# Conditional sequence block: single gathers for the first two tiles, gate weights behind them, gate matmuls as two strips inside the first layer

## The chip, the cores and the metric

The kernel runs on one core of a Trainium2 chip. The metric is the device time of one execution in microseconds (us). A run's profile shows the span from the first to the last instruction; the time of the same execution is somewhat longer. Engines are named as in the profile: PE (TensorE matmul), PEld (TensorE weight load), DVE (VectorE), ACT (ScalarE), POOL (GpSimd), SP (SyncE, which here only issues DMAs). DMA queue q1 is the one that SP issues to, q10 ACT's, q0 POOL's.

## The reference, cut to what matters

`x` is 32 x 128 x 512 float32, `t` 32 x 512, `mask` 32 x 128 (true where a position lies behind the length of its row). Everything is float32.

```python
m = mask[:, :, None]
emb = silu(t) @ ada_w + ada_b                       # 32 x 1536
shift, scale, gate_msa = split(emb, 3, axis=1)
norm = where(m, layernorm(x) * (1 + scale[:, None]) + shift[:, None], 0)
fwd = gelu(norm @ ssm_w1 + ssm_b1) @ ssm_w2 + ssm_b2    # 512 -> 512 -> 512
bwd = gelu(norm @ bwd_w1 + bwd_b1) @ bwd_w2 + bwd_b2    # the two flips cancel
x = x + gate_msa[:, None] * where(m, fwd + bwd, 0)
ff = silu(t) @ ffada_w + ffada_b
shift2, scale2, gate_mlp = split(ff, 3, axis=1)
h = gelu_tanh((layernorm(x) * (1 + scale2[:, None]) + shift2[:, None]) @ ff_w1 + ff_b1)
return x + gate_mlp[:, None] * (h @ ff_w2 + ff_b2)      # 512 -> 1024 -> 512
```

The first half changes only the tokens where the mask is true. The kernel therefore collects those tokens in 512 slots (a loop at the end takes any that are left over), computes the first half for the slots, and puts the results back; the second half is done for all 4096 tokens.

## The kernel before

**Slots.** From the mask, the kernel counts masked tokens per batch row. `edges` holds, for each row, the first slot and the one behind its last (`first`, `behind`), four times over in the 128 partitions. `pick` (128 x 512) is 1 where a slot belongs to a batch row; `pick_slots` (L212) fills half of it. `rank` (32 x 128) holds the rank of each token, and in its last column the number of the row's first token. `tokens_of` (L220) looks slots up: one matmul of `pick` with `rank` for each tile of 128 slots, a comparison with the slot number, a sum, and an addition give the token of each slot as an integer. `gather` (L239) is an indirect DMA on POOL that fetches 128 rows of `x` by these integers. The first two tiles are looked up and gathered together, the other two likewise, later.

**Modulation.** `silu(t)` is transposed to `sT` (128 x 4 x 32). `modulation_matmuls` (L259) multiplies it with the weights `ada_a`, a block of 128 input rows at a time (4 blocks) and a part j of 512 columns (0 shift, 1 scale, 2 gate); part j is written to partitions 32j to 32j+31 of a PSUM tile. `modulation_rows` (L270) adds the biases `modb_a` and so makes the rows of `mod1`. Shift and scale come first (`pm_ss`), the gate (`pm_g`) later, between transposes. `slot_part` (L287, matmul in L282) multiplies 32 rows of `pick` with 32 rows of `mod1` and gives the shift, scale or gate of each slot of a tile (`part_s` in the profile).

**First half.** `statistics` (L149) takes mean and variance (L155 to L158) and, on POOL, the inverse root (L160). `modulated` (L166) does two fused operations of 128 x 512 (L171, L172). `transposed_slots` (L175) transposes a tile in four blocks on PE and copies them with ACT. `hidden` (L182) is the first layer: 8 blocks f of 128 outputs, each 4 matmuls over 256 slots, then a Gelu on ACT with the bias `biasT`; blocks 0 to 3 use `ssm_w1` (`w1[:, :, :512]`), 4 to 7 `bwd_w1`. `project` (L196) is the second layer, `finish_slots` (L295) adds bias, gate and `x` on DVE and stores the rows in DRAM (`x1_rows`). `hidden` for the first two tiles is broken up (L614 to L625): three blocks, the gate of one tile, scale and shift of a later tile, one block, twice.

**Second half.** Two matrix products done with seven instead of eight block products, whose weight sums (`Weights.combine`, L312, and `weight_sums`, L570) DVE computes during the first half. `take_first_half` (L669) gathers the results of the first half from `x1_rows` into tiles of `x` loaded before. Statistics, normalised tiles and transposes follow, and then the block products (L905, L1091) until the end.

**What sets the order.** The opening stands in a manual schedule: each engine does its instructions in the order in which the code writes them. DMA issues wait in the same order on their engine: SP issues nearly all loads and stores, POOL the gathers and the biases, ACT the mask. A DMA also waits when it reuses one of eight completion counters (each next DMA of a kind takes the next) until the DMA before it on that counter has landed. On SP the order is: `t`, four blocks of shift and scale weights, the gate weights (1 MB, L146), then, each after a small memset on POOL that stands behind the gathers (L134), four loads of 1 MB of `w1` and `w2`; then `fw1` (2 MB, L509), `ada_f` (3 MB, L510, into the memory of `ada_a`, hence after the last gate matmul), `b2`, `b2b`, `modb_f`, `fb2`, `fw2` (2 MB, L517) and four loads of `x`. Tile pools rotate: the PSUM pools `ps_t`, `ps_h` and `ps_o` have 2, 3 and 3 banks.

```python
    mv, rstd = statistics(xc, "s01")
    xn_s = [
        modulated(
            xc[c], *rows[c], f"s{c}", xn[:, c], (mv[:, c, 0:1], rstd[:, c : c + 1])
        )
        for c in range(2)
    ]
    modulation_matmuls(pm, ada_a, 2, 3, range(2))
```

Of the kernel before, what the change touches and what calls it, by code (L numbers as in the profile page):

```python
# [22 lines left out]
def kernel(  # L23
# [89 lines left out]

    def broadcast_rows(t, vec, queue):

        n = vec.shape[0] // D
        each = t.shape[0] // n
        for j in range(n):
            queue.dma_start(
                t[j * each : (j + 1) * each, :],  # L120
                vec[ts(j, D)].rearrange("(o d) -> o d", o=1).to_broadcast([each, D]),
            )
# [8 lines left out]
    def load_blocks(t, w):  # L131
        nc.sync.dma_start(t, w.rearrange("(k p) f -> p k f", p=P))
# [5 lines left out]
    modb_a = adap.tile([3 * B, D], F32, tag="modb", name="modb_a", bufs=1)  # L138
# [7 lines left out]
    load_blocks(ada_a[:, :, 2 * D :], ada_w[:, 2 * D :])  # L146


    def statistics(src, name):  # L149

        n = len(src)
        mv = stp.tile([P, n, 2], F32, tag=f"mv{n}", name=f"mv_{name}")
        for i in range(n):
            st = stp.tile([P, 6], F32, tag="st", name=f"st_{name}_{i}")
            nc.vector.bn_stats(st, src[i])  # L155
            nc.vector.bn_aggr(mv[:, i, :], st)
        ve = stp.tile([P, n], F32, tag=f"ve{n}", name=f"ve_{name}")
        nc.vector.tensor_scalar(ve, mv[:, :, 1], EPS, None, ALU.add)  # L158
        rstd = stp.tile([P, n], F32, tag=f"rstd{n}", name=f"rstd_{name}")
        nc.gpsimd.tensor_tensor(rstd, ve, half[:, :n], ALU.pow)  # L160
        return mv, rstd
# [4 lines left out]
    def modulated(src, scale, shift, name, t, stats=None):  # L166

        if stats is None:
            mv, rstd = statistics([src], name)
            stats = mv[:, 0, 0:1], rstd  # L170
        nc.vector.scalar_tensor_tensor(t, src, stats[0], scale, ALU.subtract, ALU.mult)  # L171
        nc.vector.scalar_tensor_tensor(t, t, stats[1], shift, ALU.mult, ALU.add)  # L172
        return t

    def transposed_slots(xn, dst, name):  # L175

        ptr = ps_t.tile([P, 512], F32, tag="tr", name=f"ptr_{name}")
        for k in range(KC):
            nc.tensor.transpose(ptr[:, ts(k, P)], xn[:, ts(k, P)], ident)
        nc.scalar.copy(dst, ptr.rearrange("p (k s) -> p k s", s=P))  # L180
# [31 lines left out]
    def pick_slots(h):  # L212

        part = ts(h, NH)
        nc.vector.tensor_scalar(inside[:, part], slot_row[:, part], behind, None, ALU.is_lt)
        nc.vector.scalar_tensor_tensor(
            pick[:, part], slot_row[:, part], first, inside[:, part], ALU.is_ge, ALU.mult
        )

    def tokens_of(picked, slots, n, name, pool):  # L220

        pl = ps_t.tile([P, 512], F32, tag="tr", name=f"pl_{name}")
        for c in range(n):
            nc.tensor.matmul(pl[:, ts(c, S)], picked[:B, ts(c, P)], rank, start=True, stop=True)
        view = pl[:, : n * S].rearrange("p (c s) -> p c s", s=S)
        before = pool.tile([P, n, S - 1], F32, tag="before", name=f"before_{name}")
        nc.vector.tensor_tensor(
            before,
            view[:, :, : S - 1],
            slots.unsqueeze(2).to_broadcast([P, n, S - 1]),  # L230
            ALU.is_le,
        )
        token = stp.tile([P, n], F32, tag=f"token{n}", name=f"token_{name}", bufs=1)
        nc.vector.tensor_reduce(token, before, axis=AX.X, op=ALU.add)
        token_i = const.tile([P, n], I32, name=f"token_i_{name}")
        nc.vector.tensor_tensor(token_i, token, view[:, :, S - 1], ALU.add)
        return token_i

    def gather(dst, token_col):  # L239
        nc.gpsimd.indirect_dma_start(  # L240
            out=dst,
            out_offset=None,
            in_=x_rows,
            in_offset=bass.IndirectOffsetOnAxis(ap=token_col, axis=0),
        )
# [3 lines left out]
    def find_slots(h):  # L249
        part = slice(h * NC // 2, (h + 1) * NC // 2)  # L250
        return tokens_of(pick[:, ts(h, NH)], slot_col[:, part], NC // 2, f"s{h}", ssm)

    def gather_slots(token_i):
        both = xp.tile([P, 2, D], F32, tag="x", name=f"xc_{len(xc)}")
        for c in range(NC // 2):
            gather(both[:, c], token_i[:, c : c + 1])
            xc.append(both[:, c])

    def modulation_matmuls(pm, ada, lo, hi, blocks):  # L259
        for k in blocks:  # L260
            for j in range(lo, hi):
                nc.tensor.matmul(
                    pm[ts(j, B), :],
                    sT[:, k, :],
                    ada[:, k, ts(j, D)],
                    start=(k == 0),
                    stop=(k == KC - 1),
                )

    def modulation_rows(pm, mod, modb, lo, hi):  # L270
        rows = slice(lo * B, hi * B)
        nc.vector.tensor_tensor(mod[rows], pm[rows], modb[rows], ALU.add)

    def modulation(pm, mod, ada, modb, lo, hi):

        modulation_matmuls(pm, ada, lo, hi, range(KC))
        modulation_rows(pm, mod, modb, lo, hi)

    def of_slots(picked, c, mod, j, pool, tag, name):

        t = pool.tile([P, 512], F32, tag=tag, name=name)
        nc.tensor.matmul(  # L282
            t, picked[ts(j, B), ts(c, P)], mod[ts(j, B), :], start=True, stop=True
        )
        return t

    def slot_part(at, j, pool, tag):  # L287
        return of_slots(pick, at, mod1, j, pool, tag, f"part{j}_s{at}")
# [84 lines left out]
    upper = ssm.tile([B, 2, 4, B], BF16, name="upper")  # L373
# [48 lines left out]
    broadcast_rows(modb_a, ada_b, nc.gpsimd)  # L422
# [30 lines left out]
    pick_slots(0)  # L453

    nc.vector.tensor_scalar(rank[:, : S - 1], pg[:B, : S - 1], first[:B], None, ALU.add)

# [3 lines left out]
    nc.scalar.activation(s_sb, t_sb, AF.Silu)  # L460
    sT = ssm.tile([P, KC, B], F32, name="sT")
# [6 lines left out]

    token_i = find_slots(0)
    gather_slots(token_i)  # L470

    load_behind_gathers(w1[:, :, :D], ssm_w1)
    load_behind_gathers(w1[:, :, D:], bwd_w1)
    load_behind_gathers(w2[:, :KC], ssm_w2)
    load_behind_gathers(w2[:, KC:], bwd_w2)
    for key, vec in (("ssm1", ssm_b1), ("bwd1", bwd_b1), ("ff1", ff_b1)):
        n = vec.shape[0] // P
        nc.gpsimd.dma_start(
            bias_rows[col[key] : col[key] + n, :], vec.rearrange("(c p) -> c p", p=P)
        )  # L480
    pick_slots(1)
# [6 lines left out]
    mod1 = const.tile([3 * B, D], F32, name="mod1")  # L488
    nc.vector.tensor_scalar(modb_a[B : 2 * B], modb_a[B : 2 * B], 1.0, None, ALU.add)
    pm = ps_o.tile([P, 512], F32, tag="o", name="pm_ss")  # L490
    modulation(pm, mod1, ada_a, modb_a, 0, 2)
    rows = [(slot_part(c, 1, ps_o, "o"), slot_part(c, 0, ps_h, "h")) for c in range(2)]
    pm = ps_o.tile([P, 512], F32, tag="o", name="pm_g")
# [3 lines left out]
    mv, rstd = statistics(xc, "s01")  # L497
    xn_s = [
        modulated(
            xc[c], *rows[c], f"s{c}", xn[:, c], (mv[:, c, 0:1], rstd[:, c : c + 1])  # L500
        )
        for c in range(2)
    ]
    modulation_matmuls(pm, ada_a, 2, 3, range(2))
# [10 lines left out]
    for t, vec in ((b2, ssm_b2), (b2b, bwd_b2), (modb_f, ffada_b), (fb2, ff_b2)):  # L515
        broadcast_rows(t, vec, nc.sync)
    nc.sync.dma_start(fw2, ff_w2.rearrange("(k p) f -> p k f", p=P))  # L517
    x_of = {0: load_x(0)}
    transposed_slots(xn_s[0], xT_s[:, :, ts(0, P)], "s0")
    modulation_matmuls(pm, ada_a, 2, 3, range(2, 3))  # L520
    token_i = find_slots(1)
    gather_slots(token_i)
    transposed_slots(xn_s[1], xT_s[:, :, ts(1, P)], "s1")
    modulation_matmuls(pm, ada_a, 2, 3, range(3, KC))
# [6 lines left out]
    modulation_rows(pm, mod1, modb_a, 2, 3)  # L531

    every = ssm.tile([B, 2, P], BF16, name="every")
# [80 lines left out]
    for c in range(2):  # L614
        h1 += hidden(xT_s, NH, w1, 0, AF.Gelu, "s0", ssm, range(4 * c, 4 * c + 3))
# [21 lines left out]
    fw2_of.combine(0, 1)  # L637
# [7 lines left out]
    modulation(pm, mod2, ada_f, modb_f, 0, 3)  # L645
# [3 lines left out]
    gs = [keep_gate(c, slot_part(c, 2, ps_o, "o")) for c in (2, 3)]  # L649
# [720 lines left out]
    with tc.If(more > 0):  # L1370
# [11 lines left out]
        with tc.For_i(0, more, 1):  # L1382
# [4 lines left out]
            tok_i = tokens_of(pick_l, col_l, 1, "l", lp)  # L1387
# [7 lines left out]
            for half_no, (mod, was, wbs, bias, bcol, func) in enumerate(  # L1395
                (
                    (mod1, (ssm_w1, bwd_w1), (ssm_w2, bwd_w2), b2, col["ssm1"], AF.Gelu),
                    (mod2, (ff_w1,), (ff_w2,), fb2, col["ff1"], AF.Gelu_apprx_tanh),
# [10 lines left out]
                scale = of_slots(pick_l, 0, mod, 1, ps_o, "o", f"sc_l{half_no}")  # L1409
                shift = of_slots(pick_l, 0, mod, 0, ps_h, "h", f"sh_l{half_no}")  # L1410
# [5 lines left out]
                gate_l = of_slots(pick_l, 0, mod, 2, ps_h, "h", f"gate_l{half_no}")  # L1416
# [60 lines left out]
```

## Time and profile before

| what | value |
|---|---|
| three runs | 464.16, 466.93, 466.88 us; median 466.88 |
| the profiled execution | 463.4 us, span 461.7 us |
| busy in the span: PE, PEld, DVE | 448.6 us (97%), 364.2 (79%), 332.1 (72%) |
| ACT, POOL | 175.2 (38%), 157.8 (34%) |
| DMA | 70.41 MB, mean 153 GB/s |
| chain that ended last, by engine | PE 69%, DVE 9%, ACT 7%, POOL 5%, SP's queue 4%, issue 4% |

A timeline line gives start, length, engine, line of the code, operation, output and inputs, shapes and the number of instructions; in brackets stands the idle time of the engine before it and what ended it. A float32 matmul shows as two records. Matmul ends are modelled, so a busy PE may also be waiting. Tiles that are numbered in the code (`ssm_w1`, `h_s0`) lose their numbers in the profile; `w` is `w1` or `w2`, `fw` is `fw1` or `fw2`.

### The profile page before, as it was taken

To read this page: it belongs to the slowest core of one execution; us is meant where nothing else is said; L and a number is where in the kernel's file an instruction comes from. 1 tells how busy PE (TensorE), PEld (TensorE's weight loads), DVE (VectorE), ACT (ScalarE), POOL (GpSimd) and SP (SyncE) were. 2 spreads that over 40 slices of the span, in tenths; PEclk is the share of its full clock that TensorE was granted. 3 is DMA by queue.
4 is the path that set the end of the run, shared out by engine and by line. 5 is a ranking of instruction groups with operands and counts; after the bars stand their busy time and mean duration, and the time that the engine had idled before them with its cause. 6 is when DMAs were issued, how large, how long until landed. Compare 5 with 4: busy or idle time off the path is not lost.

```text
span 461.7 us, 5825 instructions
## 1 busy us (share of the span) xinstructions
PE 448.6 (97%) x2000; PEld 364.2 (79%) x2000; DVE 332.1 (72%) x538; ACT 175.2 (38%) x380; POOL 157.8 (34%) x153
## 2 busy tenths in 40 slices
PE   6899999999999999999999999999999999999995
PEld 2385385677888888788888888888888888888884
DVE  4649868999678839986787498867873995434645
ACT  3121021744445361344455513444455144562000
POOL 6210083048980000489700005987000025660000
PEclk9999999999999999999999999999999999999999
DMA  8999835692207734833077258220872342222022
GB/s 276 386 407 361 307 136 88 204 346 88 106 5 224 105 84 137 297 100 130 1 229 114 69 182 298 92 87 14 226 108 67 134 163 79 81 85 98 0 85 101
DMA packets 82418, 70.41 MB, mean 153 GB/s; under 512 B 63168, under 2 KB 63696, under 8 KB 81362
## 3 DMA queue, kind: packets, MB, share of 16 engines
q1 hardware_dynamic: 67298, 57.03, 39.4%
q0 software_dynamic: 4480, 11.66, 7.1%
q10 hardware_dynamic: 10608, 1.32, 2.0%
q8 instruction: 17, 0.28, 0.2%
q14 instruction: 15, 0.12, 0.1%
HBM read 56.83 MB, written 13.17 MB: 152 GB/s over the span
## 4 chain that ended last, share of the span: by engine, by line
PE 69%; DVE 9%; ACT 7%; POOL 5%; SPq 4%; issue 4%; DMA 1%; POOLq 0%; ACTq 0%; DVEq 0%
PE a_m L905 15%; PE a_o L1091 14%; PE e_m L905 12%; PE e_o L1091 12%; PE ph_s L188 6%; PE po_s L202 4%; SPq L744 4%; POOL hb L989 2%; ACT hb L867 2%; ACT xT L727 1%; DVE sx L834 1%; DVE xT L725 1%; ACT ha L867 1%; DVE xn_sy L838 1%; PE part_s L282 1%
## 5 line engine op out<-in xcount | busy, mean ns | idle before, releaser
L956 POOL TENSOR_TENSOR ha<-p_m,ha 128x512 f32<-128x512 f32 x20 | 26.9, 1345 | 152.5 <-ACT ha L963 143.3
L1091 PE MATMUL e_o<-fw,ha 128*128 128x256 f32 x256 | 57.9, 379 | 0.0
L727 ACT ACTIVATE xT<-xT,modT 128x128 f32<-128x128 f32 x112 | 44.1, 480 | 30.5 <-DMA xT<-xn 30.3
L1091 PE MATMUL a_o<-t,hb 128*128 128x256 f32 x240 | 54.1, 379 | 0.0
L1091 PEld LDWEIGHTS e_o<-fw,ha 128*128 128x128 f32 x256 | 48.6, 190 | 6.6
L1091 PEld LDWEIGHTS a_o<-t,hb 128*128 128x128 f32 x240 | 45.6, 190 | 6.2
L673 POOL DMA_INDIRECT x<-x_rows,slot_i x32 | 36.4, 1136 | 28.7 <-DMA x_rows<-t_s 18.1
L867 ACT ACTIVATE hb<-hb,biasT 128x256 f32<-128x256 f32 x64 | 29.0, 501 | 27.8 <-POOL hb L989 19.3
L956 POOL TENSOR_TENSOR hb<-p_m,hb 128x512 f32<-128x512 f32 x20 | 28.2, 1409 | 20.4 <-DVE hb L935 20.1
L919 ACT COPY p_m<-e_m 128x512 f32<-128x512 f32 x27 | 15.8, 585 | 49.2 <-PE e_m L905 46.8
L1091 PE MATMUL e_o<-fw,s 128*128 128x256 f32 x128 | 29.2, 381 | 0.5 <-DVE s L1039 0.3
L963 ACT COPY ha<-e_m 128x512 f32<-128x512 f32 x32 | 18.5, 578 | 28.0 <-PE e_m L905 27.7
L1091 PE MATMUL a_o<-t,s 128*128 128x256 f32 x128 | 28.9, 379 | 0.0
L1091 PE MATMUL a_o<-fw,ha 128*128 128x256 f32 x128 | 28.9, 379 | 0.0
L202 PE MATMUL po_s<-w,h_s 128*128 128x512 f32 x64 | 28.6, 593 | 0.0
L188 PE MATMUL ph_s<-xT_s,w 128*128 128x256 f32 x128 | 28.6, 382 | 0.0
L1091 PEld LDWEIGHTS e_o<-fw,s 128*128 128x128 f32 x128 | 24.1, 190 | 4.8 <-DVE s L1039 1.7
L188 PEld LDWEIGHTS ph_s<-xT_s,w 128*128 128x128 f32 x128 | 24.0, 190 | 4.7 <-ACT h_s L192 1.5
L1091 PEld LDWEIGHTS a_o<-t,s 128*128 128x128 f32 x128 | 24.3, 190 | 3.3
L1091 PEld LDWEIGHTS a_o<-fw,ha 128*128 128x128 f32 x128 | 24.3, 190 | 3.3
L867 ACT ACTIVATE ha<-e_m,biasT 128x256 f32<-128x256 f32 x48 | 20.0, 468 | 15.5 <-PE e_m L905 10.2
L930 DVE TENSOR_TENSOR e_m<-a_m,ha 128x512 f32<-128x512 f32 x20 | 13.9, 697 | 16.6 <-POOL ha L956 6.6
(210 smaller groups left out, 870.3 us busy)
## 6 DMA issues: line engine op xcount, KB each, us to landing
tw<-t_rows SPq DMA_DIRECT2D x16, 896.0 KB, 4.7
x<-in_x_dram SPq DMA_DIRECT2D x16, 512.0 KB, 8.4
gate<-gate_rows POOLq DMA_DIRECT2D x8, 1024.0 KB
out_dram<-x SPq DMA_DIRECT2D x15, 512.0 KB, 3.1
xT<-xn SPq DMA_DIRECT2D x92, 64.0 KB, 2.4
fw<-in_L_cond_ff_w_dram SPq DMA_DIRECT2D x2, 2048.0 KB
ada_f<-in_L_cond_ffada_w_dram SPq DMA_DIRECT2D x4, 768.0 KB, 13.7
ada_a<-in_L_cond_ada_w_dram SPq DMA_DIRECT2D x4, 512.0 KB, 5.9
```

Source lines behind the costliest of these rows:

```text
L188: nc.tensor.matmul(ph[:, :n], w[:, k, ts(f, P)], xT[:, k, :], start=(k == 0), stop=(k == KC - 1))
L202: nc.tensor.matmul(po, h[f][:, ts(i, P)], w[:, f, :], start=(f == 0), stop=(f == HC - 1))
L673: nc.gpsimd.indirect_dma_start(out=xs[i // G][i % G // 2][:, i % 2], out_offset=None, in_=x1_rows[:slots, :], in_offset=bass.IndirectOffse ...
L727: nc.scalar.activation(out, src, AF.Identity, bias=shift, scale=scale)
L744: queues[b % len(queues)].dma_start(dst[ts(q, R), b], src[ts(b, R), q])
L867: nc.scalar.activation(dst[:, n], src[:, n], AF.Gelu_apprx_tanh, bias=biasT[:, f : f + 1])
L905: nc.tensor.matmul(bank[:, ts(n, QT)], self.w_block(j, product)[:, ts(n, P)], self.x_block(j, product), start=(product in ("P1", "P5") and ...
L919: nc.scalar.copy(p5, e)
L930: nc.vector.tensor_tensor(e, a, p5, add)
L956: nc.gpsimd.tensor_tensor(self.place(RESULT[j], c), self.p5[j], other, ALU.add)
L963: nc.scalar.copy(self.place(RESULT[j], c), src)
L1091: nc.tensor.matmul(part, src[:, k, ts(i, P)], w[product][:, k, :], start=(last and k == 0), stop=True, skip_group_check=True,)
```

## The change

- The first two tiles are picked, looked up, compared and gathered each on its own (`pick_slots(ts(0, P))`, `find_slots` for one tile, `gather_slots`); the two look-up matmuls still stand together.
- The gate weights move on SP from before the gathers to behind the first half of `ssm_w1`, which alone keeps its memset on POOL. `ssm_w1` is loaded in two halves.
- The three bias vectors are loaded by ACT's queue instead of POOL's, behind the Silu.
- Statistics of tile 0 stand ahead of the addition of the shift and scale rows on DVE, those of tile 1 behind it.
- The second modulating operation of tile 1, its transposes and its copies are done in two pieces.
- The gate matmuls leave the places between the transposes. They stand between blocks 1 and 2 of the first layer and go alternately to partitions 64 to 95 and 96 to 127, so that their sum is in two strips. `mod1` and `modb_a` have 32 rows more (zeros in the bias, by a memset on DVE), and a slot's gate is a product over 64 rows, which adds the strips.
- Look-up and gathers of tiles 2 and 3 stand ahead of the transposes of tiles 0 and 1.
- `fw2` is loaded behind two of the four loads of `x`; `fw2_of.combine(0, 1)` moves behind the rows of `mod2`; the gate of tile 3 takes a bank of `ps_h`.

```diff
-    modb_a = adap.tile([3 * B, D], F32, tag="modb", name="modb_a", bufs=1)
+    modb_a = adap.tile([4 * B, D], F32, tag="modb", name="modb_a", bufs=1)
...
     ada_a = load_ada(ada_w, "a", 2 * D)
-    load_blocks(ada_a[:, :, 2 * D :], ada_w[:, 2 * D :])
...
-    def modulated(src, scale, shift, name, t, stats=None):
+    def modulated(src, scale, shift, name, t, stats=None, pieces=1):
...
-        nc.vector.scalar_tensor_tensor(t, t, stats[1], shift, ALU.mult, ALU.add)
+        for q in range(pieces):
+            part = ts(q, D // pieces)
+            nc.vector.scalar_tensor_tensor(
+                t[:, part], t[:, part], stats[1], shift[:, part], ALU.mult, ALU.add
+            )
...
+    def look_up(pl, picked, blocks):
+        for n, c in enumerate(blocks):
+            nc.tensor.matmul(pl[:, ts(n, S)], picked[:B, ts(c, P)], rank, start=True, stop=True)
+
+    def tokens_of(pl, slots, n, name):
...
+    def strip(pm, n, ada, k, j, start, stop):
+
+        nc.tensor.matmul(
+            pm[ts(n, B), :], sT[:, k, :], ada[:, k, ts(j, D)], start=start, stop=stop
+        )
...
-    broadcast_rows(modb_a, ada_b, nc.gpsimd)
+    nc.vector.memset(modb_a[3 * B :], 0.0)
+    broadcast_rows(modb_a[: 3 * B], ada_b, nc.gpsimd)
...
-    pick_slots(0)
+    pick_slots(ts(0, P))
 
     nc.vector.tensor_scalar(rank[:, : S - 1], pg[:B, : S - 1], first[:B], None, ALU.add)
-
+    pick_slots(ts(1, P))
...
+    for key, vec in bias_vecs:
+        n = vec.shape[0] // P
+        nc.scalar.dma_start(
+            bias_rows[col[key] : col[key] + n, :], vec.rearrange("(c p) -> c p", p=P)
+        )
...
-    token_i = find_slots(0)
-    gather_slots(token_i)
-
-    load_behind_gathers(w1[:, :, :D], ssm_w1)
-    load_behind_gathers(w1[:, :, D:], bwd_w1)
-    load_behind_gathers(w2[:, :KC], ssm_w2)
-    load_behind_gathers(w2[:, KC:], bwd_w2)
...
+    look_up(pl, pick, range(2))
+    for c in range(2):
+        gather_slots(both, c, find_slots(pl[:, ts(c, S)], c, 1))
+
+    load_behind_gathers(w1[:, :, : D // 2], ssm_w1[:, : D // 2])
+    load_blocks(ada_a[:, :, 2 * D :], ada_w[:, 2 * D :])
+    load_blocks(w1[:, :, D // 2 : D], ssm_w1[:, D // 2 :])
+    load_blocks(w1[:, :, D:], bwd_w1)
+    load_blocks(w2[:, :KC], ssm_w2)
+    load_blocks(w2[:, KC:], bwd_w2)
+    pick_slots(ts(1, NH))
...
+    mod = const.tile([4 * B, D], F32, name="mod1")
+    mod1 = [(ts(0, B), mod), (ts(1, B), mod), (ts(1, 2 * B), mod)]
     nc.vector.tensor_scalar(modb_a[B : 2 * B], modb_a[B : 2 * B], 1.0, None, ALU.add)
+    mv = stp.tile([P, 2, 2], F32, tag="mv2", name="mv_s01")
+    moments(xc[0], mv[:, 0, :], "s0")
     pm = ps_o.tile([P, 512], F32, tag="o", name="pm_ss")
-    modulation(pm, mod1, ada_a, modb_a, 0, 2)
+    modulation(pm, mod, ada_a, modb_a, 2)
+    moments(xc[1], mv[:, 1, :], "s1")
+    rstd = deviations(mv, "s01")
     rows = [(slot_part(c, 1, ps_o, "o"), slot_part(c, 0, ps_h, "h")) for c in range(2)]
-    pm = ps_o.tile([P, 512], F32, tag="o", name="pm_g")
+    pl = ps_h.tile([P, 512], F32, tag="h", name="pl_2")
+    look_up(pl, pick, range(2, 4))
...
+    both = xp.tile([P, 2, D], F32, tag="x", name="xc_2")
+    gather_slots(both, 0, find_slots(pl[:, : 2 * S], 2, 2))
...
+    x_of = {0: [load_side(0, 0)]}
     nc.sync.dma_start(fw2, ff_w2.rearrange("(k p) f -> p k f", p=P))
-    x_of = {0: load_x(0)}
-    transposed_slots(xn_s[0], xT_s[:, :, ts(0, P)], "s0")
-    modulation_matmuls(pm, ada_a, 2, 3, range(2, 3))
-    token_i = find_slots(1)
-    gather_slots(token_i)
-    transposed_slots(xn_s[1], xT_s[:, :, ts(1, P)], "s1")
-    modulation_matmuls(pm, ada_a, 2, 3, range(3, KC))
+    x_of[0].append(load_side(0, 1))
+    for c in range(2):
+        transposed_slots(xn[:, c], xT_s[:, :, ts(c, P)], f"s{c}", 1 + c)
...
-        h1 += hidden(xT_s, NH, w1, 0, AF.Gelu, "s0", ssm, range(4 * c, 4 * c + 3))
+        h1 += hidden(xT_s, NH, w1, 0, AF.Gelu, "s0", ssm, range(4 * c, 4 * c + 2))
+        if c == 0:
+            pm = ps_o.tile([P, 512], F32, tag="o", name="pm_g")
+            for k in range(KC):
+                strip(pm, 2 + k % 2, ada_a, k, 2, k < 2, k > 1)
+            nc.vector.tensor_tensor(mod[2 * B :], pm[2 * B :], modb_a[2 * B :], ALU.add)
+        h1 += hidden(xT_s, NH, w1, 0, AF.Gelu, "s0", ssm, range(4 * c + 2, 4 * c + 3))
...
-    fw2_of.combine(0, 1)
...
-    gs = [keep_gate(c, slot_part(c, 2, ps_o, "o")) for c in (2, 3)]
+    gs = [
+        keep_gate(2, slot_part(2, 2, ps_o, "o")),
+        keep_gate(3, slot_part(3, 2, ps_h, "h")),
+    ]
+    fw2_of.combine(0, 1)
```

## The prediction

> **What bounds the kernel now.** I read the engine totals first, then the chain of work that ended last, then the timeline of the first 90 us, then the DMA queues microsecond by microsecond.
>
> The table of stretches (columns: stretch, its length, then busy time of PE, PEld, DVE, ACT, POOL) says that TensorE is the bound once it has started:
>
> ```profile
> 20.00:25.00 5.00, 5.00 (x24) 3.57 (x23) 2.04 (x6) 1.23 (x3) 2.35 (x3) 1.00 1.05 392
> 50.00:60.00 10.00, 10.00 (x46) 4.11 (x45) 6.78 (x11) 1.17 (x2) 1.63 (x2) 1.00 0.68 258
> 60.00:70.00 10.00, 10.00 (x48) 8.81 (x47) 7.35 (x16) 2.84 (x6) 8.28 (x9) 1.00 0.29 105
> 100.00:200.00 100.00, 98.98 (x450) 84.23 (x449) 80.84 (x125) 44.38 (x98) 40.92 (x35) 1.00 0.48 142
> ```
>
> So the end moves by when the first layer (`ph_s`) starts, plus whatever work is put on PE behind that. The timeline (start, length, engine, line) shows what `ph_s` waited for:
>
> ```profile
> 7.86 1.05 POOL L240 DMA_INDIRECT xc<-in_x_dram,token_i_s  x1 [3.30 <-DVE inside L215]
> 9.22 0.97 POOL L240 DMA_INDIRECT xc<-in_x_dram,token_i_s  x1 [0.30 <-issue]
> 10.79 1.05 PE L262 MATMUL pm_ss<-ada_a,sT 128*32 128x512 f32 x4 [0.22 <-DMA ada_a<-in_L_cond_ada_w_dram]
> 11.89 0.68 DVE L272 TENSOR_TENSOR mod<-pm_ss,modb_a 64x512 f32<-64x512 f32 x1 [1.46 <-PE pm_ss L262]
> 14.03 0.69 DVE L155 BATCH_NORM_STATS2 st_s<-xc 128x6 f32<-128x512 f32 x1 [1.45 <-DMA xc<-in_x_dram,token_i_s]
> 14.55 1.90 PE L262 MATMUL pm_g<-ada_a,sT 128*32 128x512 f32 x4
> 14.86 0.66 DVE L155 BATCH_NORM_STATS2 st_s<-xc 128x6 f32<-128x512 f32 x1
> 18.30 0.75 DVE L172 SCALAR_TENSOR_TENSOR xn_s<-xn_s,rstd_s,part_s 128x512 f32<-128x512 f32 x1
> 20.38 1.04 PE L262 MATMUL pm_g<-ada_a,sT 128*32 128x512 f32 x2
> 21.59 5.45 PE L188 MATMUL ph_s<-xT_s,w 128*128 128x256 f32 x24
> 33.28 1.23 DVE L316 TENSOR_TENSOR t<-fw 128x1024 f32<-128x1024 f32 x1 [2.12 <-DMA fw<-in_L_cond_ff_w_dram]
> 52.76 3.63 PE L262 MATMUL pm_f<-ada_f,sT 128*32 128x512 f32 x24
> 58.07 1.08 POOL L673 DMA_INDIRECT x<-x_rows,slot_i  x1 [18.15 <-DMA x_rows<-t_s]
> ```
>
> VectorE idles until the first gather lands at 14.0, 5.1 us after its descriptors were written (8.91). Then it is one chain to 21.59, with gate matmuls and a look-up between the transposes. The queues say why the gather is late. From 10 to 11 us the hardware queue, still moving gate weights, has the engines to itself; from 12 to 13 the gather runs:
>
> ```profile
> q1 hardware_dynamic: 183, 0.37, 102.9%
> q0 software_dynamic: 1, 0.00, 0.1%
> ```
>
> ```profile
> q0 software_dynamic: 96, 0.34, 89.8%
> q1 hardware_dynamic: 40, 0.06, 16.2%
> ```
>
> **The change, part by part.**
>
> *Look-ups and gathers.* Compare, pick, count on 128 instead of 256: row 215 is 0.35 us at 256, row 216 0.48 at 256, and 512-wide forms of that kind take 0.74, so 1 ns an element: 0.22 and 0.35; rows 227 and 234 go from 0.42 to 0.29. Rank is ready at 4.88 instead of 5.07, the second pick at 5.48. In the new instruction order the first compare waits for both look-up matmuls, so it starts at 5.62+0.60 (row 224: 1.20 for two)+0.1=6.3, not 6.51. Token 0 is there at 7.10 instead of 7.58. Gathers are issued at 7.38 and 8.73 instead of 7.86 and 9.22: 0.5 us.
>
> *Gate weights behind them.* The mixing-weight blocks were moved by 9.0 (2.1 MB summed over q1); a gather behind an empty queue starts within 0.9 us of its descriptors (the one written at 59.15 has packets between 59 and 60). So tile 0 moves from about 9.2 to 9.9 and, with the 1.3 us between the last packets and use (12.7 to 14.0), lands at 11.2; tile 1 (written 9.70) at about 12.2. Bounds: 10.5 with no queue in front, 13.5 if the 5.1 us lag stays. I take 11.2, as the row at 12 to 13 us shows the gather at full rate as soon as q1 is empty.
>
> *New wait.* On VectorE the statistics of tile 0 now stand ahead of the addition that ends `pm_ss`. 11.2+0.93 gives 12.15 for the addition, not 11.89; the four `part_s` matmuls wait behind it. The second statistics start at 12.86 instead of 14.86.
>
> *From there to the first layer.* Before: 14.86 to the last modulation 18.30 is 3.44. Now its first half (0.48) and second (0.47), two transposes (0.33), a 256-wide copy (0.37 between 0.27 at 128 and 0.58 at 512) and hand-overs make the bias transpose free at 4.77 and `ph_s` at 5.00 after the statistics: 17.86. Its third block of rows is ready at 5.24, and is needed at 5.86. First layer 21.59-17.86=3.73 us earlier. First weights: half of `w1`, issued at 10.0, needs 2 us to start and 1.4 us of data, landed about 14; gate weights about 17, used from 21.3; nothing waits.
>
> *Strips.* Four gate matmuls leave the waiting time and go between blocks 1 and 2 on the bound engine. Row `pm_f`: 24 records in 3.56 with three strips side by side, 0.445 per pass; two strips, four passes: 1.78. Upper bound, no overlap: the row at 14.55, 1.90 for two, so 3.8. I take 1.8, nearest in form. Net so far 3.73-1.8=1.9 us.
>
> *Queues.* The three bias loads leave POOL (0.5 us each at 10.3, nothing waiting) for ACT between 3.33 and the copy of `sT` at 4.87; that copy may slip 0.3 and is wanted at 6.2. SP: `ada_f` waits for the gate strips (23 us instead of 21.45), with everything behind it; the 2 MB of `fw` keep the queue full to 33, so nothing. `fw2` behind two x loads lands near 51 and is used at 55: nothing. One more memset on DVE before 2.87: idle anyway. The subtraction moved behind `mod2` (2.45) fills DVE's idle at 55.2 (1.3) and 57.2 (1.7); nothing waits for `modT` before 80. The last gate part takes a `ps_h` bank, so its matmul need not wait for VectorE's addition at 52.94 (that addition was done before the four at 56.33 ran, 1.98 us in one go): nothing gained, and the bank is copied out before block 2 asks for it. Three memsets less on POOL (four took 0.31) and the earlier gathers let the first weights go at 10.0, not 10.49.
>
> *What is late next.* Between 9.0 and 12 q1 has nothing queued but the gathers (0.52 MB, 1.35 us): against before some 1.1 us of DMA time is lost, and the queue is full from there to 53.5. `fw` lands at about 34.3, not 33.2, and VectorE works from it without a pause: 33.28 to 52.91, less the moved 2.48, is 17.15 us, so the last addition for slots starts at 51.5, where PE alone would allow 51.0. Its store runs behind the queue's end (54.6), lands at 56.7, and the gathers start at 56.7 instead of 58.07: 1.35 earlier. That chain ends in the normalised tile at 79.46, which PE transposes at 79.50, with about 0.25 us to spare. So 1.6 of the 1.9 us are kept.
>
> The profiled execution took 463.4 (span 461.7, 1.7 around it): it would be 461.8. Runs shown are 464.16, 466.88, 466.93; against the median 466.88-1.6=**465.3 us**.
>
> [...] The early `pm_ss` passes are 0.85 us apart, `pm_f`'s 0.43, though the granted clock stands at 1.00 in both: PE warmed up near 9 us. [...]
> [...]
>
> **Rivals.**
> 1. *Slower: the gather keeps its lag.* If the 5.1 us are the gather's own, tile 0 lands at 13.5, now ahead of the `pm_ss` addition: 14.45, statistics 15.15, `ph_s` 20.15, plus 1.8 is 0.4 later than before; at 14.0 it is 0.9: 467.3 to 467.8. It decides from a landing at 13.1 (13.1+0.95+0.7+5.0+1.8=21.6). For it: the later gathers, 2.9 us from descriptors to packets at 22 to 25. Against it: that queue was full.
> 2. *Strips serial, or PE slow again.* Serial strips cost 3.8 against 3.73: no change, 466.9. Against: `pm_f`. If `ph_s` began at the pace of `pm_ss` between 6.33 and 9.0 (2.7 us at half pace), 1.35 of the 1.9 would go: 466.3. Against: PE is never idle for a whole microsecond in 14.5 to 17.9.
> 3. *Given back later.* If the queue ends 2 us later instead of 1.1, the gathers at 58.07 gain 0.5 only: 466.2. For: the queue is full to 53.5.
> 4. *More.* Tile 0 at 10.5 and no delay of the queue: addition at 11.5 to 11.9, 2.3 to 2.6 kept: 464.3.
>
> **How the numbers follow.** Forecast 0.45 (kept 1.1 to 2.2: 464.7 to 465.8), rival 1 0.17, rival 2 0.13, rival 3 0.15, rival 4 0.10. The likeliest is 465.3. The level of the runs adds to all of them: a median at the level of the profiled execution would be 461.8 with the forecast. From the lowest of that (461.3) to rival 1 on the shown median (467.7) leaves out two in ten. One per cent, 4.7 us, is about what a measurement of this kernel can tell from no change; no mechanism reaches it, so faster than that 0.11 (a low set of runs), within 0.85, slower 0.04.
>
> **What would show it.** Tile 0's statistics near 11.2 and `ph_s` near 17.9 bear out the opening; four gate strips in 1.8 us bear out the strips; `fw`'s first subtraction after 34 and the `x_rows` gather near 56.7 bear out what is lost later. A first statistics row after 13.1, a PE pause before block 2, or `ph_s` passes of 0.4 us instead of 0.2 would prove me wrong.

## The result and the profile after

| | before | after |
|---|---|---|
| median of the runs shown beside each other | 465.41 us (21 runs) | 467.30 us (21 runs) |
| lowest to highest | 463.07 to 467.85 | 464.13 to 471.60 |
| ratio after / before | | 1.0043, 95% interval 1.0026 to 1.0060 |
| profiled span | 461.7 us | 465.8 us |

The change makes the kernel 0.43% slower, about 2.0 us, where 1.6 us of gain was forecast. The two longest runs of after, 471.34 and 471.60 us, count as slow and are not in the ratio. A second measurement of the same kernel, below, gave 1.0031 (1.0007 to 1.0056).

The timeline of after, with the columns of the lines shown before:

```profile
7.52 1.05 POOL L250 DMA_INDIRECT xc<-in_x_dram,token_i_s  x1 [2.99 <-DVE before_s L237]
8.88 0.98 POOL L250 DMA_INDIRECT xc<-in_x_dram,token_i_s  x1 [0.30 <-issue]
11.03 1.05 PE L269 MATMUL pm_ss<-ada_a,sT 128*32 128x512 f32 x4 [0.58 <-DMA ada_a<-in_L_cond_ada_w_dram]
11.50 0.69 DVE L152 BATCH_NORM_STATS2 st_s<-xc 128x6 f32<-128x512 f32 x1 [0.69 <-DMA xc<-in_x_dram,token_i_s]
12.33 0.66 DVE L279 TENSOR_TENSOR mod<-pm_ss,modb_a 64x512 f32<-64x512 f32 x1
13.09 0.69 DVE L152 BATCH_NORM_STATS2 st_s<-xc 128x6 f32<-128x512 f32 x1
...
15.89 1.05 PE L187 MATMUL ptr_s<-ident,xn_s 128*128 128x128 f32 x4 [0.41 <-DVE xn_s L176]
17.13 1.18 PE L187 MATMUL ptr_s<-ident,xn_s 128*128 128x128 f32 x4 [0.19 <-DVE xn_s L176]
...
18.63 5.77 PE L198 MATMUL ph_s<-xT_s,w 128*128 128x256 f32 x16
24.34 1.91 PE L269 MATMUL pm_g<-ada_a,sT 128*32 128x512 f32 x8
...
28.23 2.18 PE L288 MATMUL part_s<-mod,pick 64*128 64x512 f32 x6
34.53 1.23 DVE L320 TENSOR_TENSOR t<-fw 128x1024 f32<-128x1024 f32 x1 [2.23 <-DMA fw<-in_L_cond_ff_w_dram]
37.45 2.18 PE L288 MATMUL part_s<-mod,pick 64*128 64x512 f32 x6
56.09 3.63 PE L269 MATMUL pm_f<-ada_f,sT 128*32 128x512 f32 x24
61.24 1.31 POOL L693 DMA_INDIRECT x<-x_rows,slot_i  x1 [20.07 <-DMA x_rows<-t_s]
```

The opening does what was forecast: tile 0's statistics move from 14.03 to 11.50 us and the first layer (`ph_s`) from 21.59 to 18.63. Yet `pm_f`, 52.76 before, begins at 56.09, 3.33 later. The table of stretches of after, for PE alone (busy time, granted clock, DMA share, GB/s), shows the first reason; before, the clock column is 1.00 in all of these stretches:

```profile
14.00:16.00 2.00, 1.59 (x11) 1.00 1.02 387
16.00:18.00 2.00, 1.81 (x8) 0.50 1.09 353
18.00:20.00 2.00, 2.00 (x7) 0.50 1.04 374
20.00:22.00 2.00, 2.00 (x6) 0.50 1.04 395
22.00:24.00 2.00, 2.00 (x8) 0.79 1.07 394
```

PE runs at half its clock from 16.0 to 22.8 us. The first 16 records of `ph_s` take 24.34-18.63=5.71 us; before, they took 5.38-1.92=3.46 (24 records less eight). The second reason stands in the groups `part_s`: six records with the gate over 64 rows take 2.11 to the next matmul (28.23 to 30.34), twice; before, 1.1 each. The sum from `ph_s` to `pm_f`: -2.96 (earlier start) +2.25 (first 16 records) +1.84 (gate strips) +2 x 1.05 (gate products) is +3.2 of the +3.33. Of the 2.25, 2.06 go away in the kernels below whose clock stays up (3.65 for 5.71); 0.19 do not.

### The profile page after: what moved, and what is told of

It is laid out like the page before. It is cut to its first block, busy times and chain, and to the rows that moved or that the text cites. A ratio compares the mean times of both kernels' runs of the same rounds, so it can differ in the third digit from the quotient of the medians.

```text
span 465.8 us, 5829 instructions
## 1 busy us (share of the span) xinstructions
PE 451.6 (97%) x2000; PEld 366.7 (79%) x2000; DVE 332.9 (71%) x545; ACT 175.4 (38%) x381; POOL 155.6 (33%) x147
## 3 DMA queue, kind: packets, MB, share of 16 engines
q10 hardware_dynamic: 10640, 1.32, 2.1%
## 4 chain that ended last, share of the span: by engine, by line
PE 77%; ACT 6%; DVE 5%; POOL 4%; DMA 4%; issue 2%; SPq 0%; DVEq 0%; POOLq 0%
PE a_o L1111 19%; PE e_o L1111 16%; PE a_m L925 14%; PE e_m L925 11%; PE ph_s L198 7%; PE po_s L212 5%; DMA tw<-t_rows 2%; PE part_s L288 2%; POOL hb L1009 2%; ACT hb L887 2%; ACT ha L887 1%; DMA xc<-in_x_dram,token_i_s 1%; POOL ha L1009 1%; ACT xT L747 1%; POOL ha L976 1%
## 5 line engine op out<-in xcount | busy, mean ns | idle before, releaser
L198 PE MATMUL ph_s<-xT_s,w 128*128 128x256 f32 x128 | 30.9, 402 | 0.0
L198 PEld LDWEIGHTS ph_s<-xT_s,w 128*128 128x128 f32 x128 | 25.4, 202 | 6.0 <-ACT gs L296 1.5
```

What stands on the lines that cost most here:

```text
L198: nc.tensor.matmul(ph[:, :n], w[:, k, ts(f, P)], xT[:, k, :], start=(k == 0), stop=(k == KC - 1))
```

## The experiments

The kernels, each by one profiled execution, but for the ratio, which is from all runs. "Half clock" is the stretch at 0.50 in the opening; "none" holds for that execution alone. "First 16" runs from the first record of `ph_s` to the next group's start (in kernels with 24 records in a row, less the 1.92 of eight); `a_m` is the first product of the second half.

| kernel | half clock | `ph_s` | first 16 | `pm_f` | `a_m` | ratio to before |
|---|---|---|---|---|---|---|
| before | none | 21.59 | 3.46 | 52.76 | 87.96 | |
| before, again | none | 21.28 | 3.46 | 52.46 | 87.71 | 463.70 us, one run |
| after | 16.0 to 22.8 | 18.63 | 5.71 | 56.09 | 91.28 | 1.0043 (1.0026 to 1.0060) |
| after, again | 18.4 to 21.8 | 18.70 | 5.16 | 55.61 | 90.81 | 1.0031 (1.0007 to 1.0056) |
| e1 filled | none | 18.33 | 3.65 | 53.73 | 90.08 | 1.0008 (0.9983 to 1.0033) |
| e10 one filler | none | 18.48 | 3.65 | 53.88 | 89.08 | 465.11 us, one run |
| e3 summed | 18.0 to 21.4 | 18.57 | 5.04 | 53.17 | 89.04 | 0.9973 (0.9953 to 0.9993) |
| e3 again | 17.1 to 20.5 | 18.28 | 4.72 | 52.56 | 88.51 | 1.0010 (0.9986 to 1.0035) |
| e4 both | none | 18.56 | 3.65 | 51.77 | 87.68 | 1.0006 (0.9982 to 1.0029) |
| e5 gate moved in before | 18.3 to 25.1 | 20.64 | 5.82 | 57.73 | 92.93 | 1.0127 (1.0089 to 1.0166) |
| e7 gate fills | none | 19.59 | 3.46 | 50.77 | 88.45 | 1.0016 (0.9995 to 1.0037) |
| e8 both, x earlier | none | 18.60 | 3.65 | 51.81 | 87.86 | 1.0041 (1.0017 to 1.0064) |
| e9 gate fills, x behind | none | 18.90 | 3.46 | 50.08 | 87.69 | 0.9999 (0.9972 to 1.0026) |

Two theories were to be told apart from their rivals: the clock falls because the gate passes left the opening, and the gate over 64 rows does not run beside the products over 32.

### e1: matmuls that nobody reads in the gate's old place

```diff
+    fill = ps_t.tile([P, 512], F32, tag="tr", name="fill")
+    strip(fill, 0, ada_a, 0, 0, True, True)
...
     look_up(pl, pick, range(2, 4))
+    strip(fill, 0, ada_a, 0, 0, True, True)
...
+        if c == 0:
+            nc.tensor.matmul(
+                fill[:B, :NH], sT[:, 0, :], ada_a[:, 0, :NH], start=True, stop=True
+            )
```

The first pass stands behind `pm_ss`, the last behind the transposes of tile 0.

> The changed kernel plus matmuls on TensorE whose output nobody reads: one 512-wide pass behind pm_ss, one behind the second look-ups, one 256-wide pass behind the transposes of tile 0. Nothing else is touched. Theory (the clock): the granted clock stays at 1.00 from 14 to 24 us, ph_s starts near 17.9 instead of 18.6, its first 16 records take 3.4 to 3.6 us instead of 5.8, and the end comes 2.3 to 3 us earlier than in the changed kernel's profile; the two gate products with 64 rows stay at 2.1 to 2.2 us. Rival (the slow first blocks wait for weights or a port, not for the clock): the 16 records still take over 5 us, and the fillers cost up to 0.6 us. Second rival (a later engine takes it back): the blocks are fast, but the end moves by under 0.7 us.

Timeline and PE stretches of e1:

```profile
18.33 3.72 PE L198 MATMUL ph_s<-xT_s,w 128*128 128x256 f32 x16
53.73 3.63 PE L269 MATMUL pm_f<-ada_f,sT 128*32 128x512 f32 x24
```

```profile
18.00:20.00 2.00, 1.91 (x10) 1.00 1.02 371
```

With more work on PE the opening is faster: the clock stays up, the 16 records take 3.65 us, and `pm_f` comes 2.36 us earlier than in after. The weights and transposes are the same, so late weights did not hold `ph_s`. The forecast of the end missed: 2.3 to 3 us earlier than after was expected, but the ratio lies only 1.35 us under the mean of the two of after, and the profiled execution took 469.61 us, the longest of its twelve. Only 1.2 of the 2.36 reach `a_m`: the load queue of e1 ran full to 60.3 us, and the gathers out of the stores behind it began at 60.71, 0.5 earlier than in after.

### e5: the kernel before with its gate passes moved

```diff
-    modulation_matmuls(pm, ada_a, 2, 3, range(2))
...
+        if c == 0:
+            pm = ps_o.tile([P, 512], F32, tag="o", name="pm_g")
+            modulation(pm, mod1, ada_a, modb_a, 2, 3)
```

The two later calls of `modulation_matmuls` go as well; the new lines stand between blocks 1 and 2 of `ph_s`.

> The kernel before, with only its eight gate matmuls' place changed: the four passes leave the time between the transposes and stand, one behind the other, between first-layer blocks 1 and 2. Gathers, loads and queues stay as before. Theory (the gate matmuls kept the clock up): ph_s starts at about 20.6 (1.0 earlier), the granted clock falls under 1.00 near 18 to 24 us, the first 16 records of ph_s take 5 to 6 us instead of 3.5, the gate passes 3.4 us more, and the end is 4 to 5 us later. Rival (the clock dip in the changed kernel comes from the earlier gathers and loads, not from the gate's absence): clock 1.00, first 16 records 3.5 us, the end 2.4 to 2.9 us later.

Timeline and PE stretches of e5:

```profile
17.23 0.66 PE L179 MATMUL ptr_s<-ident,xn_s 128*128 128x128 f32 x4 [2.00 <-DVE xn_s L172]
20.64 5.88 PE L188 MATMUL ph_s<-xT_s,w 128*128 128x256 f32 x16 [0.38 <-issue]
26.46 3.62 PE L262 MATMUL pm_g<-ada_a,sT 128*32 128x512 f32 x8
```

```profile
18.00:20.00 2.00, 1.82 (x10) 0.57 1.05 388
20.00:22.00 2.00, 1.62 (x5) 0.50 1.04 385
22.00:24.00 2.00, 2.00 (x6) 0.50 1.05 388
```

As the theory says: old gathers, old queues, and the clock falls as soon as the gate passes are gone. Here PE also stands idle for 2.00 us ahead of the dip, so this run alone does not tell missing passes of 128 rows from missing work of any kind. Serial gate passes take 3.55 us, so the strips of the change (1.84) are worth what they were forecast to be. The kernel is 5.9 us slower than before, where 4 to 5 were forecast.

### e10: one of the three unread passes

The edit is e1's pass behind the look-ups alone.

> The changed kernel with only one of the three unread passes: the 512-wide one behind the second look-ups, near 15 us (1.0 us of TensorE). If a microsecond of 128-row passes in the stretch 14 to 17 us is what the throttle asks for, the clock stays at 1.00 and the first 16 records of ph_s take 3.7 us; if the passes near 12 and 16.5 us are needed too, it drops to 0.50 for one or two stretches of 3.3 us and they take 5.0 to 5.8 us.

Timeline of e10:

```profile
15.20 1.05 PE L269 MATMUL fill<-ada_a,sT 128*32 128x512 f32 x2
18.48 3.72 PE L198 MATMUL ph_s<-xT_s,w 128*128 128x256 f32 x16
```

In this one execution the clock stayed at 1.00 with 1.05 us of a pass over 128 rows between look-ups and transposes. Whether it does so in every execution was not measured; e7 below, with its passes in the same place, speaks against it.

### e3: the strips added on VectorE

```diff
-    mod1 = [(ts(0, B), mod), (ts(1, B), mod), (ts(1, 2 * B), mod)]
+    mod1 = [(ts(0, B), mod), (ts(1, B), mod), (ts(2, B), mod)]
...
-            nc.vector.tensor_tensor(mod[2 * B :], pm[2 * B :], modb_a[2 * B :], ALU.add)
+            rows_g = ts(2, B)
+            nc.vector.tensor_tensor(mod[rows_g], pm[rows_g], modb_a[rows_g], ALU.add)
+            nc.vector.tensor_tensor(mod[rows_g], pm[ts(3, B)], mod[rows_g], ALU.add)
```

> The changed kernel, but the two gate strips are added by one more VectorE operation over 32 rows, so that the gate product reads 32 rows as before. Theory (a product over 64 rows does not run beside those over 32): the groups part_s of six records take 1.0 to 1.1 us instead of 2.1 to 2.2, twice, and the end comes 2.1 us earlier than in the changed kernel; the clock dip stays. Rival (the groups are long because they wait for the gate's sum on VectorE): they stay at 2 us or over, and with the addition more (0.6 us) the end is the same or later.

First the weight loads (PEld) of after, then the products of e3:

```profile
28.23 0.29 PEld L288 LDWEIGHTS part_s<-mod,pick 64*128 64x128 f32 x2
29.28 0.30 PEld L288 LDWEIGHTS part_s<-mod,pick 32*128 32x128 f32 x4 [0.76 <-issue]
```

```profile
27.38 0.70 PE L288 MATMUL part_s<-mod,pick 32*128 32x512 f32 x2
27.44 1.10 PE L288 MATMUL part_s<-mod,pick 32*128 32x512 f32 x4
35.57 1.13 PE L288 MATMUL part_s<-mod,pick 32*128 32x512 f32 x6
```

In after, the weights of the 32-row products are loaded only when the 64-row product is nearly done (1.05 us later); in e3 all three products overlap in 1.1. So the 64-row product, behind which the others start only at 29.3, cost 1.05 us a group here; what keeps them apart no run shows. The clock dips again, for one stretch (18.0 to 21.4 us).

> The kernel with the gate strips added over 32 rows once more, unaltered, beside the runs of the kernel before on this chip. If its lead is real the ratio is again 0.995 to 0.999; if it was a low set of runs, 0.999 to 1.003. The granted clock drops to 0.50 for one or two stretches of about 3.3 us again.

The second measurement did not bear out the first's lead: 0.9973, then 1.0010. Taken together (they are from two chips) e3 cannot be told from before, and is some 2.1 us faster than after (1.0037 less 0.9992, the means of two measurements each, of 465.5).

### e4: both

> Both of these: matmuls that nobody reads on TensorE in the opening, and the gate strips added on VectorE. If the clock and the 64-row product are the two causes and add up, the end comes 4.4 to 5.2 us earlier than in the changed kernel's profile, and against the kernel before it is 1.0 to 2.6 us earlier in the median. If one later wait (the rows of x gathered near 57 us, VectorE behind fw) takes back what the opening gains, it is within 0.5 us of the better of the two alone.

Timeline of e4:

```profile
58.12 1.37 POOL L702 DMA_INDIRECT x<-x_rows,slot_i  x1 [17.27 <-DMA t_rows<-xn_tw]
104.35 2.79 POOL L702 DMA_INDIRECT x<-x_rows,slot_i  x1 [5.76 <-DMA x<-in_x_dram]
107.45 1.72 POOL L702 DMA_INDIRECT x<-x_rows,slot_i  x1 [0.31 <-issue]
...
116.47 1.13 PE L934 MATMUL e_m<-xn_sy,tw 128*128 128x256 f32 x4 [2.93 <-DVE e_m L959]
```

The two gains add up to `pm_f` (51.77, 4.3 earlier than after). There they are taken back twice: the gathers of the first half's results begin at 58.12, as in before (58.07), and near 116 PE stands still for 2.93 us behind GpSimd, whose next gathers waited 5.76 (2.65 before) and then took 2.79 and 1.72 instead of 1.0 to 1.4. So the median is not better than e3's, and both forecasts missed: the end is neither 1.0 to 2.6 us earlier than before nor within 0.5 us of e3's 464.19, but at 466.47.

> The kernel with the unread matmuls and the summed gate once more, unaltered. In its first profile pm_f began 1.0 us earlier than before, the mixing matmuls (a_m) only 0.3 us, and TensorE then stood still for 2.9 us near 116 us behind GpSimd, which had waited 5.8 us for the next pair's x loads. Theory (an opening that gets faster runs into those loads, whose queue is full from 87 to 104 us): TensorE stands still for 1.5 to 3 us near 116 again. Rival (chance of one execution): no such gap, and a span of about 462 us.

It came again: a wait of 5.62, gathers of 2.93 and 1.72, a gap of 2.93, and 469.12 us in this one run.

### e7: the gate itself as the filler

```diff
-    load_behind_gathers(w1[:, :, : D // 2], ssm_w1[:, : D // 2])
-    load_blocks(ada_a[:, :, 2 * D :], ada_w[:, 2 * D :])
+    nc.gpsimd.memset(ada_a[0:1, 0, 2 * D : 2 * D + 1], 0.0)
+    for k in range(KC):
+        nc.sync.dma_start(ada_a[:, k, 2 * D :], ada_w[ts(k, P), 2 * D :])
+    load_blocks(w1[:, :, : D // 2], ssm_w1[:, : D // 2])
...
     look_up(pl, pick, range(2, 4))
+    pm = ps_o.tile([P, 512], F32, tag="o", name="pm_g")
+    for k in range(2):
+        strip(pm, 2 + k % 2, ada_a, k, 2, k < 2, k > 1)
```

From e3; the passes for k = 2 and 3 stand behind the transposes of tile 0, the two additions on VectorE behind the bias transpose.

> Useful work in the place of the unread matmuls: the gate weights are loaded block by block ahead of the first half of the first layer's weights, the gate's passes stand behind the second look-ups (two) and behind the transposes of tile 0 (two), and the two strips are added on VectorE over 32 rows behind the bias transpose. Theory: the granted clock stays at 1.00, nothing of the gate stands between first-layer blocks, the first 16 records of ph_s take 3.6 us, and pm_f begins 1.8 us earlier than in the kernel with the unread matmuls and the summed gate (near 50 us instead of 51.8), or 1.0 to 1.8 if the first weights, now behind 1 MB more, land after 18 us. The end, by the theory that later loads give the gain back, is no more than 1 us earlier than the kernel before; by the rival that the opening is passed on whole, 2.5 to 3 us earlier.

Timeline of e7:

```profile
17.00 1.52 PE L269 MATMUL pm_g<-ada_a,sT 128*32 128x512 f32 x4
19.59 5.45 PE L198 MATMUL ph_s<-xT_s,w 128*128 128x256 f32 x24
78.81 1.61 PE L759 MATMUL ptr<-ident,xn 128*128 128x128 f32 x4 [1.31 <-DVE xn L743]
```

`pm_f` begins at 50.77, 2.0 earlier than before, and `a_m` at 88.45, 0.5 later than before: PE now waits for the normalised tile. The load queue ran full to 59 us (53.5 before), and the stores that the gathers wait for stood in it. The ratio, 1.0016 (0.9995 to 1.0037), does not tell it from before. The profile has no dip, but other runs of e7 do lose clock (see below).

### e9 and e8: loads moved out of the way

e9 is e7 with two of the first x loads behind the stores:

```diff
-    x_of[0].append(load_side(0, 1))
...
     store_weight_sums(3)
+    x_of[0].append(load_side(0, 1))
```

> The kernel whose gate passes fill the opening, and one more edit: the last two of the first four x loads (1 MB) leave the place behind the second feed-forward weights and are issued behind the stores of t_s and of the third weight sums. In that kernel's profile pm_f began at 50.8 us, 2.0 earlier than before, but the load queue ran full to 59 us, the stores of t_s stood behind those loads, the gathers out of them began at 59.1 (before 58.1), and TensorE stood still for 1.3 us near 78 us. Theory (the queue's end gives the opening's gain back): the queue runs dry 2 to 3 us earlier, the gathers begin near 57, and a_m begins 1 to 2 us earlier than in the kernel without this edit (87.0 instead of 88.5); the median is 0.5 to 2 us earlier. Rival (GpSimd's chain, not the queue, sets it): gathers at 58 or later, a_m at 88.4 again, the same time.

Timeline of e9:

```profile
57.29 1.12 POOL L699 DMA_INDIRECT x<-x_rows,slot_i  x1 [15.78 <-DMA x_rows<-t_s]
78.06 1.61 PE L759 MATMUL ptr<-ident,xn 128*128 128x128 f32 x4 [1.25 <-DVE xn L743]
```

The queue does run dry at 54 and the gathers come 1.76 us earlier than in e7, but `a_m` (87.69) only 0.76, and `pm_f` already began 0.69 earlier in this execution, so hardly any of it is the queue's. PE still waits 1.25 for the tile, and a gap near 115 is there (1.61). 0.9999 (0.9972 to 1.0026) cannot be told from e7 or from before.

e8 is e4 with two of the next pair's x loads between the loads of summed weights:

```diff
-    for j in (1, 2):
-        now.load_weights(j)
+    now.load_weights(1)
+    x_of[1] = [load_side(1, 0, spare)]
+    now.load_weights(2)
```

> The kernel with the unread matmuls and the summed gate, and one more edit: two of the four x loads of the next pair are issued between the two loads of summed token weights instead of behind both. Theory (the next pair's x loads hold GpSimd, and GpSimd holds TensorE): GpSimd's wait for x near 100 us shrinks from 5.8 to under 3 us, the gap of TensorE near 116 us goes, and the end comes 2 to 3 us earlier than in the kernel without this edit, so 1 to 2.5 us earlier than before in the median. Rival (the second load of token weights is then late): TensorE waits for those weights near 104 us instead, and the end does not move.

Timeline of e8:

```profile
103.76 1.11 POOL L702 DMA_INDIRECT x<-x_rows,slot_i  x1 [5.00 <-DMA x_rows<-t_s]
105.18 2.03 POOL L702 DMA_INDIRECT x<-x_rows,slot_i  x1 [0.30 <-issue]
107.51 1.82 POOL L702 DMA_INDIRECT x<-x_rows,slot_i  x1 [0.30 <-issue]
```

A miss, at 1.0041 of before: the x loads were not the only thing late. The gathers now wait 5.00 for the store of the last slots, which stands in the same full queue, and the gap (1.61) remains.

### Before and after once more

> The kernel before once more, unaltered. Its first profiled execution was 2 us under the median of its runs. Theory (a gap of TensorE of 0.3 to 3 us near 116 us, behind GpSimd's gathers, and waits for token-weight rows come and go from one execution to the next in every kernel): the granted clock stays at 1.00 in the opening and ph_s begins near 21.6 again, and any difference of over 0.5 us in the span comes after 100 us. Rival (the dip of the clock comes and goes too): a clock of 0.50 somewhere between 14 and 25 us here.

Timeline of before, again:

```profile
104.85 2.43 POOL L673 DMA_INDIRECT x<-x_rows,slot_i  x1 [0.31 <-issue]
107.58 1.83 POOL L673 DMA_INDIRECT x<-x_rows,slot_i  x1 [0.30 <-issue]
114.10 1.13 PE L905 MATMUL e_m<-xn_sy,tw 128*128 128x256 f32 x4 [0.32 <-DVE e_m L930]
```

Long gathers and a small gap near 114 occur in before too; no dip of the clock does in these two profiles.

> The changed kernel once more, unaltered, on the chip and beside the runs of the kernel before that the next kernels share. Theory (the throttle decides by fixed windows of about 3.3 us, so the length of the slow stretch depends on where the opening falls in them): the granted clock drops to 0.50 again, for one such window (3.3 us) or two (6.7 us), from 16 to 18.5 us on, and the first 16 records of ph_s take 5.0 to 5.8 us; the 64-row products take 2.1 us again. Rival (the dip was chance): clock 1.00 and 3.6 us. The wait of 2.0 us for token-weight rows near 292 us in the first profile is either there again (then it belongs to the change) or gone (then it differs from run to run).

The dip is there again, one stretch of 3.4 us this time, and the 64-row products take 2.11. The wait for `tw` near 294 us, 2.04 in the first profile of after, is 0.60 here.

The record of the clock in the traces moves in fixed windows: full speed begins at 8.8 to 11.5 us (its first entry; in before at 9.34, and the 1.00 that the stretches show ahead of it is no entry), and every later change in the fourteen profiles lies a whole number of 3.413 us behind that. The first profile of after has 6.827 us at full speed, 6.827 at half and 440.319 at full speed, 2, 2 and 129 times 3.413; before has 450.559 at full speed, 132 times. So one can ask what PE did in each window. "128-row passes" are the matmuls of modulation and layers over 128 rows, and the unread ones; the rest of the busy time is look-ups, 32-row products and transposes.

| kernel | window | PE busy | of it 128-row passes | clock in the next window |
|---|---|---|---|---|
| before | 16.17 to 19.58 | 2.27 | 1.32 | 1.00 |
| e4 | 12.19 to 15.61 | 3.20 | 0.84 | 1.00 |
| e7 | 9.68 to 13.09 | 2.13 | 2.12 | 1.00 |
| after | 12.58 to 16.00 | 2.54 | 0 | 0.50 |
| after, again | 14.96 to 18.37 | 2.36 | 0 | 0.50 |
| e3 | 14.59 to 18.00 | 2.27 | 0 | 0.50 |
| e3 again | 13.65 to 17.06 | 2.41 | 0 | 0.50 |
| e5 | 14.85 to 18.26 | 1.41 | 0 | 0.50 |

A window without any 128-row pass stands ahead of each of the five dips and, up to the last windows of a run, nowhere else in the fourteen profiles. Busy time does not decide: 2.13 and 2.27 us kept the clock, 2.27 to 2.54 lost it. The length of the dip follows the same way. Where the first window at half clock held 2.19 us or more of the first layer (after again, e3 twice) full speed came back after it; with 0.78 (after) or 1.04 (e5) it came one window later.

Every execution lists its mean granted clock, profiled or not. In after it is 0.9933 (21 runs), in e3 0.9936 and 0.9932, in e5 0.9885; in before 0.9982 (29 runs), in e1 0.9987, in e4 0.9989, in e8 0.9990. The clock lost in after against before is worth 0.0049 x 466=2.3 us of PE, as an average over all runs. (Most profiles also end at half clock, for up to 2.6 us of the span; that alone leaves a mean of 0.997.)

In e7 it is 0.9968 and in e9 0.9971, though their profiles show no dip. Four of twelve runs of each are at 0.995 or lower, against 2 of 81 of before and 1 of 36 of e1, e4 and e8 together. So the gate as the filler did not keep the clock up in every execution, and part of its gain is lost again. Where in those runs the clock fell no trace shows. One place that may do it is the opening: between the last pass of `pm_ss` and the first gate pass lie 3.63 us in e7 and 3.15 in e9, about a window, and 3.48 in e10; with a pass right behind `pm_ss` (e1, e4, e8) 2.3 to 2.6, and 2.71 in before. Another is the wait near 78 us.

## Why the prediction was wrong, step by step

- *Look-ups and gathers*: right. 7.52 and 8.88 for 7.38 and 8.73; tile 0 at 11.50 for 11.2.
- *The queue in front of the gather*: right, and rival 1 fell. (The measured 467.30 is what rival 1 forecast, 467.3 to 467.8, but by luck: tile 0 did not keep its lag.) From 10 to 11 us, where q1 had the engines before, the queues of after read:

```profile
q0 software_dynamic: 66, 0.20, 62.3%
q1 hardware_dynamic: 2, 0.00, 1.1%
```

  Of the 2.53 us by which tile 0 lands earlier only 0.34 are an earlier issue. By the earlier issue alone it would have come at 13.69 (14.03-0.34).
- *New wait*: right to 0.25 us (12.33 for 12.15, 13.09 for 12.86).
- *Strips*: right. 1.84 us for 1.8, side by side; serial ones in e5 took 3.55.
- *From there to the first layer*: **this step failed.** It priced transposes and first blocks by rows at the full clock. `ph_s` began at 18.63, not 17.86 (0.23 from the later statistics; from there it took 5.54 us instead of 5.00, and 5.2 even in e4, e8 and e10, whose clock stays up, so 0.2 is a chain priced too short and 0.34 goes with transposes of 1.05 and 1.18 instead of 0.66), and its first 16 records took 2.25 more. Rival 2 had the mechanism, at 1.35 us and among 0.13 of the chances, and was dismissed with "PE is never idle for a whole microsecond in 14.5 to 17.9". That counted every kind of work as the same, and it misread the rows: before itself has a gap of 1.14 us ahead of 17.59, longer than any of after there, and keeps its clock. In the window ahead of the dip of after PE is busy for 2.54 us; before has a window with 2.27 and keeps its clock. The difference is what stands there: 128-row gate passes before, only look-ups, 32-row products and transposes after. Passes put back (e1, e4, e8), passes taken away (e5) and the windows of all profiles show it.
- *What was counted as idle*: that dismissal looked for stretches with no instruction on PE. That idle time alone decides was not shown by any run. What the runs show is that look-ups, 32-row products and transposes together, 2.54 us in a window of 3.41 in after, did not keep the clock up; none separates them. The five dips lasted 3.41 us three times and 6.83 twice.
- *The gate product over 64 rows*: a term missing from the sum. It was taken as unchanged, without a reason; it costs 1.05 us twice, 2.1 in all (e3).
- *What is late next*: right in kind. `fw` at 34.53 for 34.3. That little was to spare at the normalised tile was right: e7, with 2.0 us in hand at `pm_f`, lost all of it by `a_m`, with PE waiting for that tile. The queue's end was forecast at 54.6; it lay at 55.3 and 57.5 in the two profiles of after, and at 60.3 in e1.
- *The base*: 1.6 us were taken from the median of three runs, 466.88; the median of 21 is 465.41. Against that the forecast would have been 463.8.

With the two terms the sum would have read 3.73-0.8-2.25-1.8-2.1=-3.2 at `pm_f`, close to the -3.33 of the profile. The runs' median moved by 1.4 to 2.0 only. The two profiled executions of before took 463.4 and 463.7 us, 2 less than the median of its runs, those of after 467.6 and 468.2, 0.3 and 1.6 more than theirs; which waits make up that difference in executions without a profile is not settled.

## What to carry to other kernels

Ask of matmuls that fill a wait what they do for the clock before moving them. Here the 2.7 us of unread 128-row passes in e1 were worth 1.5 to 2 us of the work behind them, and each window of 3.41 us that held no such pass was followed by half clock. Since the windows start at a different time in each execution (the first at 8.8 to 11.5 us here), a filler should leave no stretch of that length open. A product whose row count changes is a new product: price it beside its neighbours, not alone, since 64 rows ahead of 32 cost 1.05 us more than three 32-row products together. And when an opening gets faster, look up the first chain that PE reaches with little to spare: of the 2.0 us that e7 gained up to `pm_f` nothing was left at `a_m`.

## What was not expected of the hardware

- In the profiles the half-clock stretches of the opening last 3.41 us or twice that, and begin at 16.0 to 18.4 us in different executions of much the same code. The runs of e5 must hold longer or further ones: a mean of 0.986 (the lowest of its six) loses 6.6 us, two windows in the opening and a whole one at the end lose only 5.1.
- Work that kept PE busy did not all count the same for the clock: 2.54 us of look-ups, 32-row products and transposes in a window lost it, 2.13 us with 128-row passes kept it.
- Indirect DMAs on GpSimd, 1.0 to 1.4 us each near 105 us, take 1.7 to 2.9 in some executions of the same kernel (1.12, 1.23 and 1.00 in after, 1.13, 2.43 and 1.82 in after again), beside the same unbroken run of VectorE operations. The cause was not found. All executions with a gap of over 1 us near 116 us (e1, e4 twice, e8, e9) have them; e7, as early at `pm_f`, has neither.
